# A graph layer on one Trainium2 core: fifteen groups taken straight from x, their gathers asked for in one go, no clearing by GpSimd, and one copy moved to ScalarE

## The chip, the cores and the metric

The kernel runs on one core of one Trainium2 chip. The metric is the device time of one execution in microseconds (us). Engines are named as in the profile: PE (TensorE, matrix products; PEld are its weight loads), DVE (VectorE), ACT (ScalarE), POOL (GpSimd), SP (SyncE, here a queue that issues DMAs). A letter q behind a name (SPq, ACTq) is the engine's sequencer, which issues DMAs and waits.

## What is computed

The layer norm and relu of x (12500 nodes x 128 features) is `h`. A GraphSAGE-like network over 200000 edges, sorted by destination `dst`, follows:

```
w      = edge_weight / max(wsum, EPS)[dst]            # wsum: sum of edge_weight per destination
feat   = relu(h @ W_pool + b_pool)
neigh  = segment_max(feat[src] * w, dst)              # pass 1
rst    = h @ W1_self + neigh @ W1_neigh + b1
h1     = relu(rst / max(norm(rst), EPS))
neigh2 = segment_sum(h1[src] * w, dst) / max(deg, 1)  # pass 2
out    = x + relu(h1 @ W2_self + neigh2 @ W2_neigh + b2)
```

`src` is random, so every `[src]` is a gather of 512-byte rows.

## The kernel before

**Groups.** The edges are cut into 391 groups of 512 (the last has 320). A group of sorted edges covers about 32 neighbouring nodes, since 200000 edges over 12500 nodes are 16 edges a node; the kernel gives each group a window of `LW = 48` nodes that starts at its first destination. A flag `unfit`, computed on the chip by `fitness`, sends inputs that break such assumptions to a slow branch at the end.

**Node stage** (L533 to L605, the first 97 us). A loop over 25 blocks of four 128-node tiles, four steps deep: statistics (DVE), normalising (ACT), transposing and the product with `W_pool` (PE), relu into `fr` (DVE, every fourth by ACT), store to the table `feat_d` in HBM (SP). x lies in `agg`, which SP fills with 15 DMAs at the start (L150); POOL clears each block of `agg` after its use (L563), because pass 1 later writes its windows there.

**The first groups** (`FIRST = 14`). Their rows can't be gathered from `feat_d`, which is still being written. So POOL gathers rows of x for them during the node stage (two or three of the 56 gathers a block, L588 and L446), and the features are computed anew at the beginning of pass 1: for group r, `raw_stats` and `raw_scale` (DVE), `raw_norm` (ACT, in place), `raw_columns` (PE, four transposes), `raw_back` (ACT, PSUM to SBUF), `raw_product` (PE, with `W_pool`), and the relu into `pm` (ACT, L836).

**Pass 1** (a loop over i, 103 to 1980 us). Each iteration works on several groups at once, in a hand-written order on every engine:
- POOL gathers group i from `feat_d`, four DMAs of 128 rows (L446). Every twelfth group has its first 128 rows fetched by single-row DMAs of SP and ACT (class `Rows`, L687).
- ACT scales the gathered rows (`gs`, L853) and PE transposes them into `pm` (L854). For i < FIRST the steps above stand in their place, and DVE multiplies with the weights (L874).
- DVE runs the segmented maximum of group i-1 along `pm` (L862), copies every second column to `sc` (L870), and overwrites some by `copy_predicated` (L871).
- PE transposes `sc` of group i-2 (L899), ACT copies it (`rows`, L889), DVE makes selection matrices `sel` (L882), PE multiplies (L911), and ACT copies the 48 columns into `agg` (`window_copy`, L804).
- Finished node tiles go through `nodes1` to `h_d` in HBM; a generator of small jobs for later (`side_step`) takes one step in two of three iterations.

**Buffers of the gathers.** `buffer` hands out 16 tiles in turn to the groups below 64 and 8 after that. So group 72 is the first that has to wait for the group eight before it, which is the group whose rows ACT reads at L853.

**Pass 2** (1994 to 3895 us) gathers h1 from `h_d` in the same groups, multiplies by selection matrices and adds the windows up.

The instructions of every engine run in the order of the program; semaphores make an instruction wait for another engine, and all that is behind it on its engine waits with it.

Of the kernel before, what the change touches and what calls it, by code (L numbers as in the profile page):

```python
# [18 lines left out]
P = 128  # L19
# [10 lines left out]
ROW_SHIFT = 9  # L30
BL = 8
XC = 8
FIRST = 14
RING = 8
WIDE = 2 * RING
LESS = 64
# [3 lines left out]
def gnn_kernel(ctx, tc, x, src, dst, ew, w_pool, b_pool, w1s, w1n, b1, w2s, w2n, b2, out):  # L40
# [76 lines left out]
    def buffer(g, wide):  # L117
        return ring[g % (WIDE if wide and g < LESS else RING)]
# [81 lines left out]
    sums = rp.tile([P, NT + 2], F32)  # L200
    counts = rp.tile([P, NT + 2], F32)
    heads = rp.tile([P, NT + 2], F32)
    bad = rp.tile([P, NT, 5], F32)
    for tl in (sums, counts, heads):
        nc.vector.memset(tl, 0.0)
    ones_r = rp.tile([P, G], BF16)
# [31 lines left out]
    def at_pairs(out, f, op):  # L238
        nc.vector.tensor_reduce(out, pairs(f), axis=AX.X, op=op)
# [135 lines left out]
    def fitness(get, t):  # L375

        before, cur, behind = (dr[:, t, i:i + G] for i in range(3))
        begin = work("first", 1)
        nc.vector.tensor_copy(begin, cur[:, 0:1])
        pn = beside(get, cur)  # L380
        yield
        wrong = work("goes", dtype=BF16)
        nc.vector.tensor_tensor(wrong, pn, before, OP.is_lt)
        yield
        nc.vector.tensor_reduce(bad[:, t, 0:1], wrong, axis=AX.X, op=OP.max)
        yield
        loc = work("f1")
        nc.vector.tensor_scalar(loc, pn, float(N - 1), begin, op0=OP.min, op1=OP.subtract)
        last = work("last", dtype=BF16)
        yield  # L390
        nc.vector.tensor_tensor(last, pn, behind, OP.not_equal)
        yield
        nc.vector.tensor_scalar(wrong, loc, float(LW - 1), None, op0=OP.is_gt)
        yield
        nc.vector.tensor_reduce(bad[:, t, 1:2], wrong, axis=AX.X, op=OP.max)
        yield

        one = work("one", 1)
        nc.vector.tensor_tensor(one, before[:, 0:1], behind[:, G - 1:G], OP.is_equal)
        real = work("real", 1)  # L400
        nc.vector.tensor_scalar(real, begin, float(PAST), None, op0=OP.is_lt)
        nc.vector.tensor_tensor(bad[:, t, 2:3], one, real, OP.mult)
        nc.vector.tensor_tensor(bad[:, t, 3:4], begin, need[:, t:t + 1], OP.is_lt)
        yield

        at_pairs(loc[:, :G // 2], last, OP.min)
        yield
        nc.vector.tensor_reduce(bad[:, t, 4:5], loc[:, :G // 2], axis=AX.X, op=OP.max)
# [29 lines left out]
        ne = G if g < GF else TAIL  # L438
        return *divmod(g, P), ne, [(j, min(P, ne - j * P)) for j in range(-(-ne // P))]

    def gather(gt, table_d, g, byrow=None, only=None):
        t, r, ne, chunks = edges_of(g)
        for j, k in chunks if only is None else chunks[only:only + 1]:
            if j == 0 and byrow and byrow.takes(g):
                continue
            nc.gpsimd.indirect_dma_start(  # L446
                out=gt[:k, j, :], out_offset=None, in_=table_d[:, :],
                in_offset=bass.IndirectOffsetOnAxis(ap=srcT[:k, t, j, r:r + 1], axis=0))
        return gt
# [34 lines left out]
    def raw_back(r):  # L484
        nc.scalar.activation(gts[r], raws.pop(r), AF.Copy)
# [10 lines left out]
    rest = load_rest()  # L496
    groups = list(node_groups())
    offs, rstds, pts, pfs = ({} for _ in range(4))
    raw_chunks = [(r, j) for r in range(FIRST) for j in range(Q)]

    def split_bias():

# [29 lines left out]
    for i in range(len(groups) + 3):  # L532
        at = [groups[i - k] if 0 <= i - k < len(groups) else None for k in range(4)]  # L533
        if at[3]:
            t0, n = at[3]
            pf = pfs.pop(i - 3)
            fr = wk.tile([P, Q, D], F32, name="fr", bufs=3)
            if i % 4 == 3:
                nc.scalar.activation(fr[:, :n, :], pf[:, :n, :], AF.Relu)
            else:  # L540
                nc.vector.tensor_scalar(fr[:, :n, :], pf[:, :n, :], 0.0, None, op0=OP.max)
            nc.sync.dma_start(feat_d[t0 * P:(t0 + n) * P, :].rearrange("(q p) d -> p q d", p=P),
                              fr[:, :n, :])
        if at[2]:
            t0, n = at[2]
            nc.scalar.activation(hT[:, t0:t0 + n, :], pts.pop(i - 2)[:, :n, :], AF.Copy)
            pf = pfs[i - 2] = ps.tile([P, Q, D], F32, name="pf")
            nc.tensor.matmul(pf[:, :n, :], ones_r[0:3, :P], bias_rows[0:3, :n, :], start=True, stop=False)
            for q in range(n):
                nc.tensor.matmul(pf[:, q, :], hT[:, t0 + q, :], W["pool"], start=False, stop=q == n - 1)  # L550
        if at[1]:
            t0, n = at[1]
            rstd = rstds.pop(i - 1)
            nc.vector.reciprocal(rstd, rstd)
            off = wk.tile([P, Q], F32, name="off")
            nc.vector.tensor_tensor(off, offs.pop(i - 1), rstd, OP.mult)
            xn = wk.tile([P, Q, D], F32, name="xn")
            pt = pts[i - 1] = ps.tile([P, Q, P], F32, name="pt")
            for q in range(n):
                nc.scalar.activation(xn[:, q, :], xs[:, t0 + q, :], AF.Relu, bias=off[:, q:q + 1],  # L560
                                     scale=rstd[:, q:q + 1])
                nc.tensor.transpose(pt[:, q, :], xn[:, q, :], ident)
            nc.gpsimd.memset(xs[:, t0:t0 + n, :], 0.0)  # L563
        if at[0]:
            t0, n = at[0]
            mv = wk.tile([P, Q, 2], F32, name="mv")
            if n < Q:
                nc.vector.memset(mv, 1.0)
            for q in range(n):
                st = wk.tile([P, 6], F32, name="st")  # L570
                nc.vector.bn_stats(st, xs[:, t0 + q, :])
                nc.vector.bn_aggr(mv[:, q, :], st)
            rstd = rstds[i] = wk.tile([P, Q], F32, name="rstd")
            nc.scalar.activation(rstd, mv[:, :, 1], AF.Sqrt, bias=eps)
            offs[i] = ps.tile([P, Q], F32, name="neg")
            nc.vector.tensor_scalar(offs[i], mv[:, :, 0], -1.0, None, op0=OP.mult)
        if 2 <= i < 22:
            next(first_edges, None)
        if i >= 6:
            next(rest, None)  # L580
        if i == 1:
            bias_rows = split_bias()
        if i < 2 or 9 <= i < 15:
            next(source_steps, None)
        if i >= 2:
            n = 2 + (i % 4 == 2) if i < len(groups) else len(raw_chunks)
            for r, j in raw_chunks[:n]:
                gts[r] = gather(buffer(r, True), x, r, only=j)  # L588
            raw_chunks = raw_chunks[n:]
        if i == len(groups) - 1:  # L590
            w_first, kt_first = (rp.tile([P, G], F32, name=f"r_f{k}") for k in range(2))
            kt_first = kt_first.bitcast(BF16).rearrange("p (two n) -> p two n", two=2)
            weight_rows(0, w_first)
            keep_rows(0, kt_first)
        k = i - len(groups)
        if k == 1:
            raw_scale(0)
            raw_norm(0)
            raw_columns(pq, 0)
        if k == 2:  # L600
            raw_back(0)
            raw_product(pq, 0)
            nc.scalar.activation(gts[0], raws.pop(0), AF.Relu, bias=bp_col)
            raw_scale(1)
            raw_norm(1)  # L605
        if 0 <= k < 3:
            raw_stats(k)
# [165 lines left out]
    with tc.manual_schedule(), tc.tile_pool(name="ew", bufs=3) as wk, \  # L773
# [48 lines left out]
        for i in range(max(turn) + 6):  # L822
# [10 lines left out]
            if i < FIRST:  # L833
# [6 lines left out]
                if i + 2 < FIRST:  # L840
                    raw_scale(i + 2)
                    raw_norm(i + 2)
                if i + 1 < FIRST:
                    raw_back(i + 1)

            elif i < NG:
                t, r, ne, chunks = edges_of(i)
# [11 lines left out]
            if 0 <= g < NG:  # L859
                ne = edges_of(g)[2]  # L860
                kt, pm = kts.pop(g), pms.pop(g)
                nc.vector.tensor_tensor_scan(pm[:, :ne], kt[:, :ne], pm[:, :ne], carry,  # L862
                                             op0=OP.add, op1=OP.max)
                if g + 1 < NG:
                    carry = wk.tile([P, 1], F32, name="carry")
                    nc.vector.tensor_copy(carry, pm[:, ne - 1:ne])
                sc = scs[g] = wk.tile([P, G // 2], F32, name="sc")
                two = pm[:, :ne].rearrange("p (c two) -> p c two", two=2)
                new = kt[:, :ne].bitcast(I16).rearrange("p (c two) -> p c two", two=2)
                nc.vector.tensor_copy(sc[:, :ne // 2], two[:, :, 1])  # L870
                nc.vector.copy_predicated(sc[:, :ne // 2], new[:, :, 1], two[:, :, 0])  # L871
            if i < FIRST:
                rows = gts.pop(i).rearrange("p q n -> p (q n)")
                nc.vector.tensor_tensor(pms[i], pms[i] if i else rows, ws.pop(i), OP.mult)  # L874
            node_stage(1)
            node_stage(3)
            g = i - 3
# [223 lines left out]
```

## Time and profile before

| | |
|---|---|
| median of 9 runs | 3903.34 us (3896.85 to 3908.0) |
| profiled execution | 3902.31 us, its span 3900.5 us |
| POOL busy | 2899.4 us, 74% of the span |
| PE / PEld busy | 2179.9 / 1775.9 us |
| DVE busy | 1693.4 us |
| ACT busy | 834.1 us |
| gathers from `feat_d` and `h_d` by POOL | 946 and 947 ns each, 0.3 us between two |
| granted PE clock, mean | 0.538 |

In a line of the timeline the columns are start, busy time, engine, source line, operation, what is written and read, the count, and in brackets the idle time of the engine before it with what ended it. In a line of the groups of instructions, busy time and mean duration stand behind the bar, then the idle time before them and its releasers. In the table by stretches, every engine has its busy time and, in brackets, its count; then come the granted PE clock (1.00 is full), the busy share of the 16 DMA engines and GB/s.

### The profile page before, as it was taken

To read this page: it belongs to the slowest core of one execution; us is meant where nothing else is said; L and a number is where in the kernel's file an instruction comes from. 1 tells how busy PE (TensorE), PEld (TensorE's weight loads), DVE (VectorE), ACT (ScalarE), POOL (GpSimd) and SP (SyncE) were. 2 spreads that over 40 slices of the span, in tenths; PEclk is the share of its full clock that TensorE was granted. 3 is DMA by queue.
4 is the path that set the end of the run, shared out by engine and by line. 5 is a ranking of instruction groups with operands and counts; after the bars stand their busy time and mean duration, and the time that the engine had idled before them with its cause. 6 is when DMAs were issued, how large, how long until landed. Compare 5 with 4: busy or idle time off the path is not lost.

```text
span 3900.5 us, 56561 instructions
## 1 busy us (share of the span) xinstructions
PE 2179.9 (56%) x8402; PEld 1775.9 (46%) x8402; DVE 1693.4 (43%) x4861; ACT 834.1 (21%) x2996; POOL 2899.4 (74%) x3082
## 2 busy tenths in 40 slices
PE   7754545544555545555555555555555555555555
PEld 4444444444544434444544444444444444444444
DVE  8865665666666665655752222222222222222221
ACT  7533433433433433433410000000000000000000
POOL 6777577777777777777767777777777777777776
PEclk9555555555555655555555555555555555555555
DMA  7433233333333333333322222222222222222222
GB/s 204 118 85 85 70 84 87 84 87 85 82 88 85 82 85 83 85 85 85 94 57 63 62 61 62 62 62 62 62 62 62 62 62 62 62 61 62 62 62 58
DMA packets 219430, 299.21 MB, mean 77 GB/s; under 512 B 68045, under 2 KB 142362, under 8 KB 219052
## 3 DMA queue, kind: packets, MB, share of 16 engines
q0 software_dynamic: 97536, 199.88, 20.5%
q1 hardware_dynamic: 112716, 92.65, 8.3%
q10 hardware_dynamic: 8800, 3.00, 0.3%
q14 instruction: 306, 2.51, 0.2%
q8 instruction: 72, 1.18, 0.1%
HBM read 275.49 MB, written 19.77 MB: 76 GB/s over the span
## 4 chain that ended last, share of the span: by engine, by line
issue 27%; DMA 26%; DVE 13%; PE 13%; SPq 7%; POOL 5%; ACT 4%; ACTq 4%; POOLq 0%; DVEq 0%
DMA gt<-h_d,srcT 16%; DVE pm L862 5%; SPq L687 5%; POOL gt L446 5%; PE pm L854 4%; DMA kt<-keep_d 3%; DMA ga<-feat_d 3%; PE pa L970 3%; ACTq L687 3%; ACT gs L853 2%; SPq L683 2%; DVE sc L870 1%; PE pn L724 1%; DVE sc L871 1%; DVE sel L882 1%
## 5 line engine op out<-in xcount | busy, mean ns | idle before, releaser
L446 POOL DMA_INDIRECT gt<-h_d,srcT x1515 | 1433.2, 946 | 478.8 <-issue 346.6
L446 POOL DMA_INDIRECT gt<-feat_d,srcT x1375 | 1302.2, 947 | 446.9 <-issue 215.5
L970 PE MATMUL pa<-s,gt 128*128 128x48 f32 x3030 | 971.0, 423 | 832.1 <-DMA gt<-h_d,srcT 742.6
L970 PEld LDWEIGHTS pa<-s,gt 128*128 128x128 f32 x3030 | 758.4, 313 | 1045.9 <-DMA gt<-h_d,srcT 834.4
L854 PE MATMUL pm<-ident,gs 128*128 128x128 f32 x1507 | 454.1, 434 | 792.9 <-DVE sc L871 435.0
L979 DVE TENSOR_TENSOR agg<-pa,agg 128x48 f32 x391 | 81.4, 208 | 1472.2 <-PE pa L970 1047.6
L854 PEld LDWEIGHTS pm<-ident,gs 128*128 128x128 f32 x1507 | 274.5, 199 | 906.5 <-ACT gs L853 437.4
L862 DVE TENSOR_TENSOR_SCAN pm<-kt,carry,pm 128x512 f32<-128x512 bf16 x389 | 497.7, 1279 | 367.4 <-DMA kt<-keep_d 288.4
L853 ACT ACTIVATE gs<-gt,ewT 128x128 f32<-128x128 f32 x1375 | 439.5, 391 | 168.2 <-DMA ga<-feat_d 147.4
L911 PEld LDWEIGHTS pa<-sel,rows 128*128 128x128 f32 x1556 | 345.3, 307 | 52.4 <-ACT agg L804 50.7
L911 PE MATMUL pa<-sel,rows 128*128 128x48 f32 x1556 | 352.3, 371 | 17.4 <-ACT agg L804 15.7
L899 PE MATMUL pr<-ident,sc 128*128 128x128 f32 x782 | 234.1, 400 | 0.0
L882 DVE TENSOR_SCALAR sel<-cols,lastT,invT 128x48 f32<-128x48 f32 x782 | 212.4, 325 | 0.0
L871 DVE COPY_PREDICATED sc<-kt,pm 128x256 f32<-128x256 int16 x389 | 172.2, 443 | 13.2
L889 ACT ACTIVATE rows<-pr 128x256 f32<-128x256 f32 x392 | 143.6, 367 | 107.2 <-PE pr L899 107.2
L899 PEld LDWEIGHTS pr<-ident,sc 128*128 128x128 f32 x782 | 163.2, 218 | 0.1
L870 DVE COPY sc<-pm 128x256 f32<-128x256 f32 x391 | 162.1, 415 | 0.0
L952 DVE TENSOR_TENSOR s<-hit,w2T 128x192 f32<-128x192 f32 x391 | 139.8, 358 | 13.5
L950 DVE TENSOR_TENSOR hit<-iota,locT 128x192 f32<-128x192 f32 x391 | 139.4, 357 | 0.8
L673 DVE TENSOR_SCALAR ri<-ri 1x128 int32<-1x128 int32 x78 | 18.6, 238 | 269.2 <-DMA ri<-in_src 268.5
L804 ACT ACTIVATE agg<-pa 128x48 f32 x389 | 78.7, 202 | 209.7 <-PE pn L720 196.8
L735 ACT ACTIVATE sq<-r 128x128 f32<-128x128 f32 x98 | 29.7, 304 | 261.7 <-DVE r L731 261.6
(228 smaller groups left out, 1709.8 us busy)
## 6 DMA issues: line engine op xcount, KB each, us to landing
kt<-keep_d SPq DMA_DIRECT2D x194, 256.0 KB
ga<-h_d SPq DMA_DIRECT2D x3072, 0.5 KB
ga<-h_d ACTq DMA_DIRECT2D x3072, 0.5 KB
ga<-feat_d SPq DMA_DIRECT2D x2880, 0.5 KB
gt<-h_d,srcT POOLq DMA_INDIRECT x1515
gt<-feat_d,srcT POOLq DMA_INDIRECT x1375
ga<-feat_d ACTq DMA_DIRECT2D x960, 0.5 KB
h_d<-h SPq DMA_DIRECT2D x98, 64.0 KB
```

What stands on the lines that cost most here:

```text
L446: nc.gpsimd.indirect_dma_start(out=gt[:k, j, :], out_offset=None, in_=table_d[:, :], in_offset=bass.IndirectOffsetOnAxis(ap=srcT[:k, t, j, ...
L687: eng.dma_start(ga[r + k:r + k + 1, :], self.bytes[None, bass.ds(at[k], 4 * D)])
L853: nc.scalar.activation(gs[:k, j, :], rows_j, AF.Copy, scale=ewT[:k, t, j, r:r + 1])
L854: nc.tensor.transpose(pms[i][:, j * P:j * P + k], gs[:k, j, :], ident[:k, :k])
L862: nc.vector.tensor_tensor_scan(pm[:, :ne], kt[:, :ne], pm[:, :ne], carry, op0=OP.add, op1=OP.max)
L870: nc.vector.tensor_copy(sc[:, :ne // 2], two[:, :, 1])
L871: nc.vector.copy_predicated(sc[:, :ne // 2], new[:, :, 1], two[:, :, 0])
L882: nc.vector.tensor_scalar(sels[g][:k, j, :], cols[:k, 1, :], lastT[:k, t, j, r:r + 1], invT[:k, t, j, r:r + 1], op0=OP.is_equal, op1=OP.mult)
L889: nc.scalar.activation(rws[g][:k, j, :], pr[:k, j, :], AF.Copy)
L899: nc.tensor.transpose(prs[g][:k, j, :], sc[:, j * P:j * P + k], ident)
L911: nc.tensor.matmul(pas[g], rows[:k, j, :], sel[:k, j, :], start=j == 0, stop=j == len(chunks) - 1)
L970: nc.tensor.matmul(pas[g], rows_j, s[:k, j, :], start=j == 0, stop=j == len(chunks) - 1)
```

## The change

- POOL no longer clears `agg`. DVE clears its first 48 columns once. In `fitness`, two more columns of `bad` are set where the next group's first node lies more than 48 behind this group's, or this group's more than 48 behind the last node of the group before: four small DVE instructions and one more step of the side jobs for each of the four blocks of 128 groups.
- `FIRST` is 15 in place of 14. The 60 gathers from x are asked for in two bunches: twelve groups behind block 1 of the node stage, three behind block 15.
- For the first groups, the copy of every second column to `sc` is made by ACT, not DVE. On DVE the product with the weights moves ahead of `copy_predicated`; on ACT, `raw_back` moves behind the copy.

```diff
-FIRST = 14
+FIRST = 15
...
-    bad = rp.tile([P, NT, 5], F32)
+    bad = rp.tile([P, NT, 7], F32)
...
+        yield
+        after = work("after", 1)
+        nc.vector.tensor_scalar(after, behind[:, G - 1:G], float(N), begin, op0=OP.min, op1=OP.subtract)
+        nc.vector.tensor_scalar(bad[:, t, 5:6], after, float(LW), None, op0=OP.is_gt)
+        nc.vector.tensor_tensor(after, begin, before[:, 0:1], OP.subtract)
+        nc.vector.tensor_scalar(bad[:, t, 6:7], after, float(LW), None, op0=OP.is_gt)
         yield
...
-            nc.gpsimd.memset(xs[:, t0:t0 + n, :], 0.0)
...
-        if i >= 2:
-            n = 2 + (i % 4 == 2) if i < len(groups) else len(raw_chunks)
-            for r, j in raw_chunks[:n]:
-                gts[r] = gather(buffer(r, True), x, r, only=j)
-            raw_chunks = raw_chunks[n:]
+        if i == 15:
+            nc.vector.memset(agg[:, :LW], 0.0)
+        if i in (1, 15):
+            for r in range(FIRST):
+                if (r < WIDE - NT) == (i == 1):
+                    gts[r] = gather(buffer(r, True), x, r)
...
                 if i + 2 < FIRST:
                     raw_scale(i + 2)
                     raw_norm(i + 2)
-                if i + 1 < FIRST:
-                    raw_back(i + 1)
...
-                nc.vector.tensor_copy(sc[:, :ne // 2], two[:, :, 1])
+                if i < FIRST:
+                    nc.scalar.activation(sc, two[:, :, 1], AF.Copy)
+                    rows = gts.pop(i).rearrange("p q n -> p (q n)")
+                    nc.vector.tensor_tensor(pms[i], pms[i] if i else rows, ws.pop(i), OP.mult)
+                else:
+                    nc.vector.tensor_copy(sc[:, :ne // 2], two[:, :, 1])
                 nc.vector.copy_predicated(sc[:, :ne // 2], new[:, :, 1], two[:, :, 0])
-            if i < FIRST:
-                rows = gts.pop(i).rearrange("p q n -> p (q n)")
-                nc.vector.tensor_tensor(pms[i], pms[i] if i else rows, ws.pop(i), OP.mult)
+            if i == 0:
+                nc.vector.tensor_tensor(pms[0], gts.pop(0).rearrange("p q n -> p (q n)"), ws.pop(0), OP.mult)
+            if i + 1 < FIRST:
+                raw_back(i + 1)
```

More of the change, by code (lines that the diff above doesn't have):

```diff
@@ L439, in edges_of, with gather @@
         return *divmod(g, P), ne, [(j, min(P, ne - j * P)) for j in range(-(-ne // P))]
-    def gather(gt, table_d, g, byrow=None, only=None):
+    def gather(gt, table_d, g, byrow=None):
         t, r, ne, chunks = edges_of(g)
-        for j, k in chunks if only is None else chunks[only:only + 1]:
+        for j, k in chunks:
             if j == 0 and byrow and byrow.takes(g):
@@ L498, in gnn_kernel @@
     offs, rstds, pts, pfs = ({} for _ in range(4))
-    raw_chunks = [(r, j) for r in range(FIRST) for j in range(Q)]
     def split_bias():
```

## The prediction

> **What bounds the kernel now.** I read the page first, then the waits and the timeline of POOL, and then the stage that the change rewrites.
>
> ```profile
> PE 2179.9 (56%) x8402; PEld 1775.9 (46%) x8402; DVE 1693.4 (43%) x4861; ACT 834.1 (21%) x2996; POOL 2899.4 (74%) x3082
> ...
> L446 POOL DMA_INDIRECT gt<-feat_d,srcT x1375 | 1302.2, 947 | 446.9 <-issue 215.5
> ```
>
> POOL issues a gather in 0.95 us and pauses 0.30 us before the next, so 1.252 us each. That is its whole rhythm from 102 us to the end, and 74% busy means that it nearly always gathers. If this were all, a gather less would be 1.25 us less, and the change takes four `feat_d` gathers from POOL. But POOL stops three times early in pass 1:
>
> ```profile
> 385.73 0.95 POOL L446 DMA_INDIRECT gt<-feat_d,srcT  x1 [0.30 <-issue]
> 406.79 0.95 POOL L446 DMA_INDIRECT gt<-feat_d,srcT  x1 [20.12 <-ACT gs L853]
> ...
> 452.33 0.95 POOL L446 DMA_INDIRECT gt<-feat_d,srcT  x1 [5.78 <-ACT gs L853]
> ...
> 512.50 0.95 POOL L446 DMA_INDIRECT gt<-feat_d,srcT  x1 [1.70 <-ACT gs L853]
> ```
>
> These are the gathers of groups 72, 80 and 92. Each needs the buffer that ACT empties at L853 for the group eight before: 64, 72 and 84. Without its normal 0.30 pauses POOL loses 26.7 us there. After 512 us it never stops again until pass 1 is gathered (1978 us), and pass 2 is gathered without a stop too. So the end of the kernel hangs on when ACT reaches group 84, at 512 us; what POOL saves before that is waited away. That front of ACT, DVE, PE and SP ("the consumers") is what has to be costed. It starts with the first groups:
>
> ```profile
> 158.40 0.66 ACT L836 ACTIVATE pm<-pq,bp_col 128x512 f32<-128x512 f32 x1 [1.76 <-PE pq L490]
> ...
> 164.49 0.66 ACT L836 ACTIVATE pm<-pq,bp_col 128x512 f32<-128x512 f32 x1 [3.02 <-PE pq L490]
> ```
>
> ```profile
> 165.18 0.70 DVE L874 TENSOR_TENSOR pm<-pm,gs 128x512 f32<-128x512 f32 x1 [2.73 <-ACT pm L836]
> ```
>
> ACT waits for PE's product at every relu (L836), and at the end of the stage DVE waits for ACT. DVE was full (5.55 us from scan to scan, no gap) only because it started the stage late; a loop ACT-PE-ACT is the slower one: relu, four normalisations, `raw_back`, `rows`, window copy, PE's L911, PE's product, next relu. Its relus start at 103.73, 123.19 (group 5), 164.49 (group 12) and 168.04 (group 13): 4.87 us a step for four steps, where window copy and L911 are not yet in the loop, then 41.30 over 7 steps, 5.90 each, and a short last step of 3.55.
>
> The product's length follows the granted clock. Table by stretches, the products alone:
>
> ```profile
> 97.00:124.00 27.00, 10.38 (x10) 2.51 (x10) 0.50 0.48 147
> 124.00:128.00 4.00, 1.09 (x2) 0.30 (x2) 0.93 0.33 81
> 128.00:141.00 13.00, 4.08 (x4) 1.09 (x4) 0.50 0.50 130
> ```
>
> A pair of matmuls (one group) takes 2.04 us at clock 0.50 and 1.09 at 0.93. Steps with the slow pair are 6.09 us long, those with the fast one 5.3 to 5.5.
>
> **The change part by part.**
>
> *No clearing.* 24 memsets of 0.53 to 0.55 us and one of 0.33, with 0.16 before each, leave POOL: about 17 us. Worth nothing by itself: the 26.7 us of stops at 387 to 512 us cover it. If they were gone, it would still be covered, because the gathers from `feat_d` can't start before the last store of the table, issued at 94.91; the first such store took 4.0 us (27.73 to 31.73 in the chain of waits), and POOL starts them at 101.56. At most 2.7 us could come of it.
>
> *Four gathers less from `feat_d`* (5.0 us): covered by the same stops, nothing.
>
> *The bunch at block 1.* Its first gather needs only `srcT`, ready at 11.3 us, so POOL issues from 11.4 on instead of 16.28, without memsets between: some 13 gathers instead of 7 by 27 us. The DMA engines are full in most of that time, and they delay a store:
>
> ```profile
> 20.00:30.00 10.00, 9.54 (x37) 7.03 (x36) 6.23 (x26) 5.23 (x13) 7.19 (x9) 1.00 1.13 310
> ```
>
> ```profile
> 31.82 0.69 DVE L541 TENSOR_SCALAR fr<-pf 128x512 f32<-128x512 f32 x1 [4.93 <-DMA feat_d<-fr]
> ```
>
> The last line is the only long stop of the node stage: DVE waits until the first table store has left `fr`, and that store stands in SP's queue behind the 15 loads of x, all issued by 27 us. Six gathers more are 384 KB: 1.2 us at the 310 GB/s of the row, 1.6 at the 235 of the first 50 us; some fit in before 18 us, where the engines had room. I take +1.2; 0 if they fit into gaps, 2.5 if the stores suffer as well. Later the queues hold about the same rate as before (0.8 gathers a us), so no more. The second bunch waits for nothing long: 48 gathers end near 72 us, when block 15 is past.
>
> *The copy on ACT.* Nearest row: ACT's own 128x256 copy from PSUM (L889), 0.37 us, the next ACT instruction 0.26 behind its start; DVE's copy is 0.415. So 0.26 to 0.42, I take 0.30. In ACT's order it stands between `raw_norm` and `raw_back`, both in the loop above, so nothing hides it and it can't be below nothing. It waits for DVE's scan of group i-1; behind it on ACT stand `raw_back`, `rows`, the window copy and the square root of `raw_stats`; PE's product waits for `raw_back`, and DVE's `copy_predicated` (behind it `sel` and the next statistics) for the copy. What DVE saves (0.45 a step from start to start) lies beside a loop that is longer: nothing.
>
> *A fifteenth group.* One step of the loop more, one group of the ordinary kind less, which costs DVE 2.62 to 3.12 us there (scans 14 and 15). At step 11 the square root for group 14 is new; it waits for DVE at about 5 us of the step, and behind it ACT loads indices (0.7) and issues four row DMAs (1.5) before the next relu: 7.3 instead of 6.4, +0.9.
>
> The sum, from the relu of group 1: four steps of 4.87 + 0.35 (here the square root, which ends 5.2 into the step, sets it) make 20.9; eight of 5.90 + 0.30 make 49.6; +0.9; the short one 3.55 + 0.30. The relu of group 14 comes at 103.73 + 75.2 = 178.9, and scan 14, 1.73 later as scan 13 did (168.04 to 169.77), at 180.7. Before it was 172.89: **+7.8 us**. The clock decides its bounds. With the fast product throughout, statistics and square root set steps of 5.3: 12 of them and 3.85 put scan 14 at 172.9, no change. With the slow one always, eight steps of 6.39 in place of 6.20 are 1.5 more, +9.3.
>
> On the clock a rule speaks against the change. The rows: clock 0.50 from 97 us on, 0.93 in single stretches of some 4 us; PE was busy 3.32 us of the 3.40 before the one at 124 us. I stay with the mix of these rows. The Trainium skill (TensorE: Matmul & The Clock Gate, "What's actually happening") has it that the half rate is the default and that a busy window of about 3.4 us lifts it, which fits the row. Longer steps with the same matmuls would by that page earn fewer fast windows, and with none of them the stage would cost +9.3 instead of +7.8.
>
> *Does the delay arrive at group 84?* From 170 us DVE is full, at 204 us it waits 8.37 us for an index that SP issues late: SP's single-row DMAs set the pace then. They share the delay since SP's rows wait for the row DMAs that ACT issues at the end of iterations 11 to 14. SP may win some back there; I take 0.8 off. From group 24 to 84 ACT comes by every 58 to 60 us per twelve groups with POOL 40 to 60 us ahead, so nothing there absorbs a delay, and POOL's last stop moves with it.
>
> *Small things.* The memset of 48 columns (under 0.17 us, L146 clears 128 in that), and 16 small DVE instructions of at most 0.17 in the side jobs, 2.7 us, spread over iterations in which DVE idles and POOL is 30 us ahead; 2.7 if that lead were gone.
>
> Total: +1.2 + 7.8 - 0.8 = **+8.2 us**, 3902.3 to 3910.5 for the profiled execution; that one lies 1.0 under the median, so **3911.5** for the median of runs. What a measurement of this kernel can tell from no change is about 0.2%, 7.8 us, so the forecast is just "slower".
>
> **The rivals.**
> 1. *ACT keeps up and DVE's relief counts.* The 67.5 us from scan 0 to scan 13 lose 13 copies of 0.41 and gain a step of 5.14: scan 14 at 169.6 instead of 172.89, -3.3; with +1.2 of the store, 3901.2. Not slower. It holds if the product is mostly fast (1.09), so that the loop is below 5.3. For it: DVE was gapless until 159. Against: the three ACT and DVE rows above. Half-way between this and the forecast lies 3906, still "same". Together 0.41.
> 2. *POOL decides after all*: 5.0 us of gathers and 2.7 from the earlier start are kept: 3895.6, just inside or just beyond 0.2%. It decides only if ACT were at group 64 before POOL asks for 72, near 379 us; ACT is there at 405.83. 0.08, with anything unforeseen that speeds up the consumers.
> 3. *The change doesn't do what it says*: a gap raises the flag and the slow branch runs, thousands of us. 512 edges cover about 32 nodes, 48 are allowed: 0.01.
>
> **How the numbers follow.** Slower by over 0.2%: 0.50 (the forecast, with the slow-clock end, the larger store stall and 2.7 us of side jobs: 3911 to 3918). Within 0.2%: 0.41. Faster: 0.09. The likeliest case alone spans 3907 to 3917; to leave out no more than two in ten the range takes in rival 1 and half of rival 2: 3899 to 3919.
>
> **What would show it.** Right: relu starts 6.2 us apart for groups 5 to 13 and ACT waiting for the product; DVE waiting for ACT's copy before `copy_predicated`; scan 14 some 9 us later; DVE's stop at 32 us over 5.5; POOL still stopping for L853 at groups 72 to 92, and some 15 us longer in sum (8 later, 5 and up to 2.7 earlier there), with POOL idle before its first `feat_d` gather. Wrong: steps of 5.1 with a full DVE, the stop at group 72 gone, or a last stop that does not move with scan 14.

## The result and the profile after

The changed kernel takes **3913.16 us** (median of 10 runs, 3910.85 to 3917.43) against 3903.45 us for the kernel before (30 runs): ratio **1.0026, 95% interval 1.0019 to 1.0034**, 9.7 us more. In another job, with its own runs of the kernel before, the ratio was 1.0020 (1.0011 to 1.0029). The forecast was 3911.5 us and "slower", just beyond what can be told from no change; so it came.

Every experiment below is compared with runs of the kernel before in its own job. In the last two jobs all kernels, the one before too, took some 45% longer, with long pauses between SP's single-row transfers (the last section has what the traces show of them); their ratios stand by themselves.

The page of the changed kernel, POOL's share and its gathers from `feat_d`:

```profile
PE 2191.5 (56%) x8404; PEld 1784.9 (46%) x8404; DVE 1690.1 (43%) x4875; ACT 839.3 (21%) x3013; POOL 2885.7 (74%) x3057
...
L453 POOL DMA_INDIRECT gt<-feat_d,srcT x1375 | 1301.6, 947 | 453.1 <-issue 233.5
```

POOL works 13.7 us less and the kernel is longer, as step one of the prediction has it. The timeline of POOL shows where the relief went:

```profile
100.62 0.95 POOL L453 DMA_INDIRECT w2T<-feat_d,srcT  x1 [13.74 <-issue]
...
413.73 0.94 POOL L453 DMA_INDIRECT gt<-feat_d,srcT  x1 [23.05 <-ACT gs L857]
...
458.98 0.95 POOL L453 DMA_INDIRECT gt<-feat_d,srcT  x1 [5.52 <-ACT gs L857]
...
519.69 0.95 POOL L453 DMA_INDIRECT gt<-feat_d,srcT  x1 [2.18 <-ACT gs L857]
```

The first line is POOL idle for 13.74 us ahead of its first gather from the table: the work saved before, waited away. The other three are the old stops (20.12, 5.78 and 1.70 us), the last one now at 519.69 in place of 512.50. The front that they wait for is 7.2 us later; that is most of the result.

DVE's stop for the first store of the table:

```profile
33.75 0.69 DVE L547 TENSOR_SCALAR fr<-pf 128x512 f32<-128x512 f32 x1 [7.21 <-DMA feat_d<-fr]
```

It was 4.93 at 31.82. (In before_again, the second trace of the kernel before, it is 6.44 us long at 31.34, so the prediction's sign, a stop of over 5.5 us, tells little; where the stop ends is compared further down.) And one whole step of the groups from x, first ACT, then PE within it:

```profile
146.17 0.66 ACT L842 ACTIVATE pm<-pq,bp_col 128x512 f32<-128x512 f32 x1 [1.11 <-PE pq L497]
146.75 1.64 ACT L483 ACTIVATE lastT<-lastT,raw_off,raw_rstd 128x128 f32<-128x128 f32 x4
148.29 0.37 ACT L875 ACTIVATE sc<-pm 128x256 f32<-128x256 f32 x1
148.55 0.58 ACT L492 ACTIVATE locT<-pn 128x512 f32<-128x512 f32 x1
149.03 0.38 ACT L899 ACTIVATE rows<-pr 128x256 f32<-128x256 f32 x1
149.29 0.21 ACT L810 ACTIVATE agg<-pa 128x48 f32 x1
151.19 0.30 ACT L469 ACTIVATE raw_rstd<-raw_mv,eps 128x4 f32<-128x4 f32 x1 [1.68 <-DVE raw_mv L467]
152.59 0.66 ACT L842 ACTIVATE pm<-pq,bp_col 128x512 f32<-128x512 f32 x1 [1.10 <-PE pq L497]
```

```profile
149.56 1.09 PE L921 MATMUL pa<-sel,rows 128*128 128x48 f32 x4 [2.21 <-ACT agg L810]
150.45 2.04 PE L497 MATMUL pq<-locT,w_pool 128*128 128x512 f32 x2
```

Read the starts: relu 146.17, normalise 146.75, copy 148.29, `raw_back` 148.55, `rows` 149.03, window copy 149.29, PE from 149.56 to 152.49, the next relu at 152.59. There is no gap in this ring; what stands in brackets is one engine waiting for the other. The copy holds 0.26 us of it, from its start to that of `raw_back`. A step is 6.42 us; the prediction's step with the slow product was 6.39. The slow step of the kernel before was 6.09, so 0.33 came on: 0.26 is the copy, and 0.07 more lies between the starts of the window copy and of the next relu (3.29 us against 3.22), for which the profile shows no cause.

DVE, which was to be relieved, waits for ACT instead (waits of DVE, 125 to 180 us; total, times, longest):

```profile
DVE sc L880 <- ACT sc L875: 6.6, 7, 1.1
```

### The profile page after: what moved, and what is told of

It is laid out like the page before. It is cut to its first block, busy times and chain, and to the rows that moved or that the text cites. A ratio compares the mean times of both kernels' runs of the same rounds, so it can differ in the third digit from the quotient of the medians.

```text
span 3910.2 us, 56546 instructions
## 1 busy us (share of the span) xinstructions
PE 2191.5 (56%) x8404; PEld 1784.9 (46%) x8404; DVE 1690.1 (43%) x4875; ACT 839.3 (21%) x3013; POOL 2885.7 (74%) x3057
## 4 chain that ended last, share of the span: by engine, by line
issue 28%; DMA 26%; PE 12%; DVE 12%; SPq 8%; ACT 5%; POOL 5%; ACTq 4%; POOLq 0%; DVEq 0%
DMA gt<-h_d,srcT 15%; SPq L693 5%; DVE pm L866 5%; POOL gt L453 5%; DMA kt<-keep_d 4%; PE pm L858 4%; DMA ga<-feat_d 4%; PE pa L980 3%; ACTq L693 3%; ACT gs L857 2%; SPq L689 2%; DMA gt<-feat_d,srcT 1%; ACTq L689 1%; PE pn L730 1%; DVE sc L880 1%
## 5 line engine op out<-in xcount | busy, mean ns | idle before, releaser
L962 DVE TENSOR_TENSOR s<-hit,w2T 128x192 f32<-128x192 f32 x391 | 139.8, 357 | 13.5
```

## The experiments

The measured values together; relus 5 to 11 as mean step, starts of scan 14, of `gs` of group 84 and of pass 2's first gather, all from one trace each:

| run | ratio to before (95%) | step | scan 14 | gs 84 | pass 2 |
|---|---|---|---|---|---|
| before | - | 5.87 | 172.89 | 511.54 | 1994.44 |
| changed kernel, first trace | 1.0026 (1.0019-1.0034) | 6.18 | 184.64 | 518.73 | 2004.25 |
| before_again | - | 5.88 | 173.97 | 509.32 | 1988.61 |
| after_again | 1.0020 (1.0011-1.0029) | 6.27 | 185.53 | 518.03 | 1998.09 |
| dve_copy | 1.0014 (1.0005-1.0023) | 5.59 | 180.05 | 514.22 | 1993.03 |
| back_first | 1.0029 (1.0019-1.0040) | 6.18 | 186.28 | 518.88 | 1997.97 |
| first14 | 1.0018 (1.0009-1.0027) | 6.18 | 179.60 | 515.18 | 1994.43 |
| paced | 1.0022 (1.0013-1.0031) | 6.16 | 180.72 | 513.75 | 1993.32 |
| paced_full | 1.0020 (1.0011-1.0029) | 5.95 | 183.58 | 515.59 | 1995.90 |
| before11 | 0.9994 (0.9985-1.0003) | 5.44 (5 to 10) | 166.46 | 501.74 | 1983.60 |

One ratio is known to 3.5 us; single traces vary by 2 to 3 us late in the kernel. So the steps are judged by the early columns, the time by the ratio. The runs dve_copy, back_first, first14 and paced are of one job on one chip, the two repeats, paced_full and before11 of another job on another chip.

**The two kernels again.**

> The kernel before, unchanged, for a trace from the same chip as the other runs. All theories: scan 14 at 173 us, POOL's last stop for L853 near 512 us. Open: whether scan 84 comes 298 us after scan 24 as in its first trace; the changed kernel and all its variants needed 294 to 296 there.

> The changed kernel, unchanged, on the same chip as the variants: 9 to 10 us over the kernel before (ratio 1.0025). Scan 14 at 184 to 185 us, gs of group 84 near 518.5. The stops of POOL after 1300 us (1.92 us at 1700) are chance if they are not seen again.

`gs` of group 84 stands 8.7 us later in the changed kernel, pass 2 9.5 us. Scan 84 came 294.9 us after scan 24 in this trace of the kernel before, so the 298.0 of its first trace was not repeated. The changed kernel's stop at 1700 us did not come back; another, of 1.48 us, stood at 579.

**The copy given back to DVE** (dve_copy):

```
-                    nc.scalar.activation(sc, two[:, :, 1], AF.Copy)
+                    nc.vector.tensor_copy(sc, two[:, :, 1])
```

> The changed kernel (3913.2 us) with the copy of a group of x given back to DVE; the place of raw_back, the fifteen groups and the gathers stay as changed. Theory A (the loop ACT-PE-ACT sets the steps of the groups from x, and the copy on ACT adds 0.30 to 0.35 us to each): the first five steps go from 5.1 back to 4.9 us, the later ones from 6.42 to 6.1, the relu of group 14 comes some 4 us earlier (178.4 instead of 182.4), and the time is 3909.2. Theory B (DVE is as full as ACT and the copy was a relief for it): DVE gets 0.42 us a step back, the steps are as long or longer, and the time is 3913 to 3919.

The relu of group 14 came at 177.80 in place of 183.27 in after_again (178.4 expected), the time was 5.2 us over the kernel before in place of 7 to 10. Theory A; theory B wanted longer steps. DVE has the copy back and the steps are shorter. One slow step, ACT's relus of groups 6 and 7:

```profile
133.10 0.66 ACT L842 ACTIVATE pm<-pq,bp_col 128x512 f32<-128x512 f32 x1 [0.55 <-PE pq L497]
...
139.19 0.66 ACT L842 ACTIVATE pm<-pq,bp_col 128x512 f32<-128x512 f32 x1 [1.19 <-PE pq L497]
```

It is 6.09 us, as in the kernel before; back_first, first14 and paced, in the same job with the copy on ACT, have 6.39 to 6.43. So 0.33 of the 0.68 us by which the mean steps of dve_copy and after_again differ is the copy. The rest is that three of the six steps here had a faster product, and one in after_again; whether the edit has part in that is not shown. The ratio's interval overlaps that of the changed kernel, so the gain is shown in the steps, not in the time.

**`raw_back` early again** (back_first):

```
                     raw_norm(i + 2)
+                if i + 1 < FIRST:
+                    raw_back(i + 1)
...
-            if i + 1 < FIRST:
-                raw_back(i + 1)
             node_stage(1)
```

> The changed kernel (3913.2 us) with raw_back put back to its old place, before the copy on ACT. Theory A: the copy still stands on ACT ahead of rows and the window copy, which PE's product waits for through L921, so the steps stay at 6.4 us and the time within 1 us of 3913. Theory C (it is the place of raw_back behind the copy that lengthens the loop, since the copy itself waits for DVE's scan and raw_back with it): the steps go back to 6.1 us and the time to 3909.

Not faster: steps of 6.18, ratio 1.0029. The place of `raw_back` is not the cost. But the waits, 125 to 180 us, of ACT and then of DVE, changed:

```profile
ACT raw_rstd L469 <- DVE raw_mv L467: 17.3, 8, 2.3
```

```profile
DVE sc L882 <- ACT sc L877: 8.4, 9, 1.6
```

The copy comes later, DVE's statistics with it, and ACT waits longer for them at the square root (17.3 us against 13.5). So a second ring, ACT's copy, DVE's statistics, ACT's square root, lies close behind the first. The prediction named these links and let the square root set the early steps, at 5.22 us; that a later copy lengthens them it did not have: two of the four are 5.68 us here, where the changed kernel has 5.22 and 5.20.

**Fourteen groups of x** (first14), in the changed kernel:

```
-FIRST = 15
+FIRST = 14
```

> The changed kernel (3913.2 us) with fourteen groups of x instead of fifteen. Theory A: one step of 6.42 us less in the loop, one ordinary group of 2.6 to 3.1 us more, and POOL's four gathers more (5.0 us) are covered by its stops at groups 72 to 92: scan 14 comes 3.4 us earlier, POOL's stop at group 72 is 8 us shorter (5.0 by work, 3.4 by ACT), the time is 3909.8. Theory D (POOL's work decides): 5.0 us more, 3918.

Scan 14 is 5.9 us earlier than in after_again and 5.0 earlier than in the first trace of the changed kernel (3.4 expected), `gs` of group 84 2.9 and 3.6 earlier (3.4 expected), the time 6.6 us over the kernel before. Theory A; the four gathers more from `feat_d` cost nothing that shows, against theory D, which wanted some 15 us over the kernel before (the interval ends at 10.5). As with dve_copy, the interval overlaps that of the changed kernel.

**POOL paced as before** (paced, then paced_full with the full clearing): the old interleaving of the gathers with the blocks, and behind the transposes of a block a memset:

```
-        if i in (1, 15):
-            for r in range(FIRST):
-                if (r < WIDE - NT) == (i == 1):
-                    gts[r] = gather(buffer(r, True), x, r)
+        if i >= 2:
+            n = 2 + (i % 4 == 2) if i < len(groups) else len(raw_chunks)
+            for r, j in raw_chunks[:n]:
+                gts[r] = gather(buffer(r, True), x, r, only=j)
+            raw_chunks = raw_chunks[n:]
...
+            nc.gpsimd.memset(xs[:, t0:t0 + n, :1], 0.0)
```

with `:` in place of `:1` in paced_full.

> The changed kernel (3913.2 us) with POOL paced as before: the gathers of x issued two or three a block, and between them a memset of one column of the block of x just used, which makes POOL wait for ACT as the old clearing did. Theory A (the bunch of early gathers holds up the loads of x and the first stores of the table): DVE's stop for the first store goes from 7.2 back to 4.9 us, the node stage ends 2.9 us earlier and scan 0 is at 102.3 to 103.3; the time is 3910.3. Theory E (the delay of the node stage comes from the new work of the flag in the side jobs, or from chance): scan 0 stays at 106 and the time at 3913.

> As the run with POOL paced by small memsets, but with the full clearing memsets of the kernel before (24 of 0.53 us and one of 0.33), so that POOL gets back 13 us and more of work ahead of its first gather from feat_d. Theory A (the clearing was hidden by POOL's stops at groups 72 to 92): the same time as with the small memsets, 8 to 9 us over the kernel before, and the stop at group 72 shorter by what POOL starts later. Theory D (POOL's work decides): 5 to 13 us slower than with the small memsets.

In paced, DVE's stop for the first store:

```profile
32.14 0.69 DVE L548 TENSOR_SCALAR fr<-pf 128x512 f32<-128x512 f32 x1 [5.87 <-DMA feat_d<-fr]
```

The instruction behind this stop started at 33.1 to 34.3 us in all five traces with the early bunch and at 31.3 to 32.1 in the five without it (the two of the kernel before, before11, paced, paced_full). The bunch costs 1.9 us there on average. Scan 0 of paced came at 102.41, as theory A had it, against 105.3 to 106.2 with the bunch; that of paced_full came at 106.01 without the bunch, for a reason that follows. In paced the gain lasted to pass 2, which began 4.8 us earlier than in after_again; the ratio did not show it (1.0022), so what the bunch costs at the end stays open. paced_full gave the same ratio as paced although its POOL reaches the table much later than in the changed kernel (100.62):

```profile
108.62 0.95 POOL L453 DMA_INDIRECT w2T<-feat_d,srcT  x1 [0.30 <-issue]
```

That is eight microseconds later, and 4.9 later than in paced, with no loss in the time, as far as the ratios tell: POOL's work before the stops is worth nothing, and theory D's 5 to 13 us are excluded but for their lower end. The stop at group 72 did not shrink by the 4.9 us (23.21 against 23.77 in paced): POOL waited 2.5 us less at 167 to 180 us, and the front came 1.8 us later. (The node stage of paced_full lost 3.7 us against paced between blocks 5 and 23, 57.1 us in place of 53.4. There PE was late: from 38 to 97 us its granted clock was 0.88, in paced 1.00, in the eight other traces 0.91 to 1.00. The clearing alone doesn't do that: with the same clearing, both traces of the kernel before and before11 took 53.6 to 55.4 us for that stretch, the five of the changed kernel with the early bunch 54.4 to 54.9.)

**Fewer groups of x** (before11), in the kernel before:

```
-FIRST = 14
+FIRST = 11
```

> The kernel before with eleven groups of x instead of fourteen, nothing else. Theory A (the loop ACT-PE-ACT of the groups from x is slower than the ordinary groups by some 3.3 us a group, and POOL's extra gathers, 3 x 5.0 us, are covered by its 26.7 us of stops at groups 72 to 92): scan 14 comes 9 to 10 us earlier, at 163 to 164 us, POOL's stops shrink from 26.7 to some 2 us, and the time is 9 us under the kernel before (ratio 0.9977). Theory D (POOL's work decides): 15 us slower. Theory F (the ordinary groups can't start that early, since the first gathers from feat_d start at 101.6 us whatever is done): no gain or a loss, with ACT waiting for gathered rows at group 11.

POOL's timeline of before11:

```profile
99.61 0.95 POOL L446 DMA_INDIRECT invT<-feat_d,srcT  x1 [6.14 <-issue]
...
442.61 0.94 POOL L446 DMA_INDIRECT gt<-feat_d,srcT  x1 [3.12 <-ACT gs L853]
...
502.70 0.94 POOL L446 DMA_INDIRECT gt<-feat_d,srcT  x1 [1.65 <-ACT gs L853]
...
856.76 0.94 POOL L446 DMA_INDIRECT gt<-feat_d,srcT  x1 [1.59 <-ACT gs L853]
```

The stop at group 72 is gone, that at 80 is 3.12 us in place of 6.32 in before_again, that at 92 is 1.65, not smaller than the 1.39 there. The front is 7.5 us earlier at scan 14, where theory A wanted 9 to 10, and 7.6 at group 84. Theory F's wait at group 11 is not in the trace: ACT starts `gs` of that group at 153.18 without a gap. The time does not follow theory A: 2.8 us under the kernel before, the interval reaching from 5.8 under to 1.2 over. In the trace the 7.6 are 5.0 at pass 2 (a late stop of 1.59, gathers 1.2 us longer in sum), 3.6 at the last gather (gathers 1.4 longer) and 1.2 at the end (the last gather ends 12.7 us before the span does, not 10.4). The late stop may belong to the kernel; the longer gathers and the longer end may be chance (first14 had such an end as well, 12.5 us), which one trace can't show. That this version beats the kernel before is not shown; the changed kernel it beats.

**All three costly parts undone** (combo14: the edits of dve_copy, back_first, first14 and paced together; combo11 and combo12 with that many groups in place of fourteen; combo11_b is combo11 in another job).

> All three costly parts of the change undone at once: copy on DVE, raw_back early, fourteen groups, POOL paced by one-column memsets; what is left of the change is that nothing is cleared by POOL (13 us of work less) and that the flag covers the gaps. Theory A: copy, fifteenth group and early bunch make the whole difference, so scan 14 is at 172 to 174 us and the time within 3 us of the kernel before (ratio 0.9995 to 1.0005). Theory D (POOL's work decides, and its relief was hidden by the other parts): 5 us or more under the kernel before.

> As the run with all three parts undone, but with eleven groups of x. Theory A: gs of group 84 comes at 500 to 502 us, 8 us before that of the kernel before, POOL's stops nearly vanish, and the time is 6 to 9 us under the kernel before (ratio 0.998). Theory G (what is gained at group 84 is lost again later in pass 1, since ACT then waits for the rows that SP fetches): ratio 0.999 to 1.0005, with stops of POOL of over 1 us after 520 us.

> The same with twelve groups of x. Theory A: two groups of x less than before give 6.6 us at scan 14, POOL's extra gathers (10.0 us) are covered by its stops (26.7 us), some 10 us of stops are left, and the time is 5 to 6 us under the kernel before (ratio 0.9985). Theory G: as with eleven.

> The same kernel as the run before with eleven groups and all three parts undone, once more, since the runs of that job had single-row transfers of SP with pauses of 1 to 4 us between them, so that all kernels, the one before too, took 45% longer and SP set their pace. With the rows as in the other runs, theory A: gs of group 84 at 500 to 503 us, some 8 us before that of the kernel before, POOL's stops at groups 72 to 92 down to 2 to 6 us, the time 4 to 9 us under the kernel before (ratio 0.998 to 0.999). Theory G (given back later): ratio 0.9995 to 1.0005.

Ratios 1.0018 (1.0007 to 1.0029), 1.0034 (1.0020 to 1.0048), 1.0046 (1.0028 to 1.0063) and 1.0029 (1.0017 to 1.0040), where the kernel before took 5647 us and, for the last, 5719. No theory had this. SP's timeline, combo14 and then before_again, shows another bound:

```profile
708.04 14.91 SPq L696 DMA_DIRECT2D ga<-feat_d  x16
...
726.24 15.80 SPq L696 DMA_DIRECT2D ga<-feat_d  x16
```

```profile
738.09 7.51 SPq L687 DMA_DIRECT2D ga<-feat_d  x16
745.94 0.36 SPq L527 DMA_DIRECT2D kt<-keep_d  x1
747.17 6.66 SPq L687 DMA_DIRECT2D ga<-feat_d  x16
```

Sixteen row transfers take twice as long to issue, POOL waits 937 us in all for ACT's `gs` (L862) in combo14, and nothing that the earlier theories weigh is the bound. Scan 24 comes at 282.1 us with fourteen groups of x and at 299.6 with eleven. Why combo14 is slower than the kernel before there was not traced, and whether combo14 equals the kernel before under the conditions of the other jobs stays open.

## Why the prediction was right, point by point

*The mechanism*: POOL's relief is worth nothing and the loop of the groups from x sets when ACT reaches group 84. Shown: the first by paced_full and first14, to within some 5 us, the second by dve_copy and first14, in the steps, at scan 14 and at group 84. In the time only the whole change is clear of noise; no single part is, and a run that undoes all parts under the same conditions is missing.

*The loop*: predicted 75.2 us from the relu of group 1 to that of group 14; measured 74.85 and 76.53 (after_again). Its terms: early steps 5.22 predicted, 5.08 measured; slow steps 6.39 against 6.42; step 11 7.3 against 7.44; the copy 0.30 against 0.26 by starts and 0.33 by the slow steps. Scan 14 stood 2.26 behind the last relu, not 1.73. From the relu of group 1 to scan 14 the changed kernel took 8.0 us longer in the first pair of traces and 9.6 in the second; 7.8 was predicted. The Trainium skill (ScalarE: Activation LUTs, "What ACT_TABLE_LOAD costs") gives an ACTIVATE with immediate scale and bias 186 ns and 0.833 ns an element, with some 93 ns of overlap between neighbours. By it the copy would be estimated at 0.40 us long and 0.31 of the ring; the trace has 0.37 and 0.26, and that decides.

*The clock*: the products alone, changed kernel and then the one before. The columns are the length of the stretch, PE, its weight loads, DVE, ACT (the relus that read the products), then as in the prediction's table by stretches:

```profile
128.00:170.00 42.00, 12.72 (x14) 3.21 (x14) 0.00 (x0) 4.46 (x7) 0.62 0.42 111
```

```profile
124.00:168.00 44.00, 14.06 (x16) 3.64 (x16) 0.00 (x0) 4.61 (x7) 0.61 0.42 114
```

A group's pair costs 1.82 us and 1.76: granted clock 0.62 and 0.61. The mix stayed as it was, as I assumed; the loss of all fast stretches, which the prediction weighed after the Trainium skill (TensorE: Matmul & The Clock Gate, "What's actually happening"), did not come.

*The store*: +1.2 predicted, bounds 0 to 2.5; 1.9 at the stop. At the relu of group 1 it was 3.8 us in the first pair of traces and 1.9 in the second. The term was too small.

*The win-back*: 0.8 predicted between the groups of x and group 84. The delay at scan 14 was 11.7 and 11.6 us, at `gs` of group 84 7.2 and 8.7: 4.6 and 2.9 came back. This is the term that was mis-sized most. Of the 4.6, some 3 come from the first trace of the kernel before, which took 298.0 us from scan 24 to 84 in place of 294.9. The rest lies between scans 15 and 84, where the prediction has SP's rows set the pace; which row releases it was not tried.

*After 520 us*: I took the delay as fixed from the last stop on. It grew by 2.6 us in the first pair and 0.8 in the second, through late stops of which the longest is not repeated:

```profile
1700.11 0.95 POOL L453 DMA_INDIRECT gt<-feat_d,srcT  x1 [1.92 <-ACT gs L857]
```

Store, loop, win-back and late growth make 3.8 + 8.0 - 4.6 + 2.6, 9.8 us, in the first pair and 1.9 + 9.6 - 2.9 + 0.8, about 9.5, in the second; the prediction had 1.2 + 7.8 - 0.8. That the sum came out so well (+8.2 against +9.7 and +7.6 of the medians) is in part luck: too small a store and too small a win-back cancel.

*What failed outright*: "some 15 us longer in sum" for the three stops. They are 30.75 us, 3.15 longer. The missing part stands at 146 to 180 us, a wait that I did not look for (POOL's waits, 130 to 600 us):

```profile
POOL locT L453 <- ACT pm L842: 4.4, 2, 3.0
...
POOL w2T L453 <- ACT pm L842: 3.1, 1, 3.1
...
POOL lastT L453 <- ACT pm L842: 1.7, 1, 1.7
...
POOL invT L453 <- ACT pm L842: 1.2, 1, 1.2
```

With POOL earlier and the groups of x later, POOL finds the ring's buffers still held by groups of x, whose relu (L842) frees them: these five stops and one of 1.33 us at 174.19, for which the profile names no releaser, are 9.95 us without the normal pauses. The account closes: 7.2 (the front later) + 5.0 (gathers saved) + 0.9 (start at 100.62, not 101.56) = 13.1 = 3.15 + 9.95.

*The rivals*: ACT keeping up fell with dve_copy and with DVE's waits; POOL deciding fell with first14 and paced_full; the raised flag would have cost thousands of us. One rival no run takes alone, the flag's new instructions on DVE. In the changed kernel they run between 1418 and 1648 us (L407 to L410), so they have no part in the 7.2 us at group 84; a part in the late growth is not excluded.

## What to carry to other kernels

Before giving an idle-looking engine a copy, write down the ring that sets the step, start by start; here ACT was 21% busy over the kernel, and yet the ring through it and PE had no gap. An engine that is the busiest over the whole span can still have its savings waited away at one place; find its last stop and cost what that stop waits for. And a gain at the bound must be followed to the end of the kernel: of 7.6 us at group 84 in before11, 1.2 were left in its trace and 2.8 in the median of its runs.

## What the runs showed of the hardware

In the two jobs that took 45% longer, it is the queues that issue the single-row transfers that are slow. A register move, an instruction that transfers nothing, stands ahead of every transfer in the same queue; in before_again and then in combo14 (shortest, median and longest in ns):

```profile
L687 SPq MOVE ga<-feat_d x2880: 29/29/38, 153.0 to 1910.9; - x192
```

```profile
L696 SPq MOVE ga<-feat_d x2880: 2/29/1460, 186.3 to 2846.2; - x192
```

In combo14, 950 of SP's 5954 moves and 290 of ACT's 4034 took 0.5 us or more, in before_again none. The packets of 512 bytes, the size of a row, took 27 ns in the median in both traces. So the transfers themselves are not slower, but the instructions that ask for them come more slowly. Why is not shown: the two jobs ran on other chips than the experiments above, so a trait of a chip and a passing state can't be told apart, and of the kernel before there is only the time under these conditions.

From one row transfer of SP to the next, 790 of the 5951 steps in before_again took 1 to 4 us, in combo14 1989, with the median issue at 0.228 us in both; for most of these pauses the profile names no releaser. Under these conditions eleven groups of x instead of fourteen, which brought the front forward otherwise, put scan 24 back by 17.5 us.
